# Moving ten steps of each row's relu experts from the second part of a slot to the first part of the next

## The chip, the cores and the metric

The kernel runs on one core of one Trainium2 chip. The metric is the device time of one execution in microseconds (us). TensorE is called PE here, VectorE DVE, ScalarE ACT, GpSimd POOL and SyncE SP, as in the profile. All data are 32 bit floats.

## The reference, cut to what matters

The input is a batch of 4 rows of 512 tokens with 128 channels. Two layers follow each other. Each adds an attention and a mixture of experts to its input, both taken from the same layer norm:

```python
xn = _layernorm(x, axis=-1)
x = x + _L0_attn_ref(xn, ...) + _L0_ffn_ref(xn, ...)
xn = _layernorm(x, axis=-1)
x = x + _L1_attn_ref(xn, ...) + _L1_ffn_ref(xn, ...)
```

The first attention is banded: for 16 heads each token looks back at 64 tokens, through two GELU networks on differences of projections. The first layer's experts are 16 gated ones, of which a token uses 4. The second attention is full, with 16 heads of 8 channels over the row's 512 tokens. The second layer's experts, the "relu experts" of this study, are these:

```python
for e in range(N_EXPERTS):            # 8
    h = jax.nn.relu(xf @ W1[e] + b1[e])   # 128 -> 512
    y = h @ W2[e] + b2[e]                 # 512 -> 128
    out = out + gate[:, e:e + 1] * y
```

All experts are computed for every token, and the gate of those that the router doesn't choose is zero.

## The kernel before, in words

The work is written as Python generators, the tracks. A track issues some instructions and yields; what lies between two yields is a step. `woven` runs several tracks side by side: each comes with a quota, and the track that is least far on in its share of the quota does the next step. A track leaves when it ends or when it has used up its quota, and it can be taken up again later. A scheduler then sets the final order of the instructions on each engine. It starts from the order written, looks at which tiles are free, and can move instructions past each other; matmuls of the scores, of `lbank` (L586) and of the second attention's weighting (L879) have a high priority in it. On the chip each engine works through its own queue in order.

The first layer goes through four slots, one for each row b. A slot has two parts, and each is one `weave`:

- `band_logits(b)` has 66 steps, 64 of which subtract two windows on DVE (L572, the tile `z`), apply GELU on ACT (L574, L578), and multiply on PE with four column tiles side by side (L586, into `lbank`). The last step writes the exponentials `e` (L628, L632) to a table `by_t` in HBM (L633). 30 steps are in the first part (24 for row 0), the others in the second.
- `gated_experts(b)` has 16 experts with two matmuls of 128x512 (L686, L693) and four pairs of 128x128 (L675).
- `band_values(b - 1)`, in the first part, reads `by_t` (L312), transposes (L321), writes to a second table `by_s` (L327), reads that in another shape (L339) and multiplies with the values (L353, L357).
- `prepare(b + 1)`, in the second part, makes the next row's layer norm, projections and routes.
- `relu_experts(b - 1)` starts in the second part of slot b and goes on in the first part of slot b + 1. It needs the whole first layer of row b - 1.

`relu_experts` has 43 steps in the slots. Six make the layer norm, the transpose (L235), the router (four matmuls of `hidden`, L388, and 16 small ones, L418), the routes and `total`. 36 steps belong to nine passes of four: in each of them one `hidden` of expert e (L388 on PE, then a relu on ACT, L396) and one product of expert e - 1 (L454). At the head of a pass come the loads of the two weights and of the route (L440, L442, L444, all issued by SP, into tiles with two buffers each), at its end a product on DVE (L458) and a sum on POOL (L459). The last step adds the sum to the row. In the attention stage a step of `hidden` and one of L454 are apart, so what is left of a row there counts twice.

After the four slots comes the attention stage. `full_attention` works on pairs of score matmuls: in each of its inner steps one pair of heads is multiplied for the maxima (L966, then L983 on DVE) and one pair for the weights (L966, then the exponential L990 on ACT), and in between come the products with the values (L879), transposes (L815) and projections. Its score matmuls are held in a written order, the list `pace`, and the experts' `hidden` is tied to it. Beside it run, in this order, `band_values` of the last row together with the rest of row 2's relu experts, and then all of row 3's.

Of the kernel before, what the change touches and what calls it, by code (L numbers as in the profile page):

```python
# [29 lines left out]
B, T, C = 4, 512, 128  # L30
# [49 lines left out]
def woven(*tracks):  # L80


    live = [[g, n, 0] for g, n in tracks]
    while live:
        t = min(live, key=lambda v: (v[2] + 1) / v[1])
        t[2] += 1
        if next(t[0], "end") == "end" or t[2] == t[1]:
            live.remove(t)
        yield
# [8 lines left out]
def two_layers(ctx: ExitStack, tc: tile.TileContext, w: dict, consts: bass.AP, out: bass.AP):  # L98
# [8 lines left out]
    def bank():  # L107
        return ps_f.tile([P, 512], FP, tag="f", name="bank")
# [16 lines left out]
    def c_(name):  # L125
        return cst[:, offs[name][0]:offs[name][1]]
# [80 lines left out]
    def layernorm(b, dst, pin=False):  # L207

        mv = small.tile([P, TPB, 2], FP, tag="mv", name="mv")
        for i in range(TPB):  # L210
            st = small.tile([P, 6], FP, tag="st", name="st")
            ins = nc.vector.bn_stats(st, x1[:, b * TPB + i, :])
            if pin and not i:
                tc.keep_in_program_order(ins)
            nc.vector.bn_aggr(mv[:, i, :], st)
        rs = inv_sqrt(mv[:, :, 1], 1.0)
        for i in range(TPB):
            nc.vector.tensor_scalar(
                dst[:, i, :], x1[:, b * TPB + i, :], mv[:, i, 0:1], rs[:, i:i + 1],
                ALU.subtract, ALU.mult,  # L220
            )
# [9 lines left out]
    def transposed(src):  # L231

        pt = bank()
        for i in range(TPB):
            nc.tensor.transpose(pt[:, i * P:(i + 1) * P], src[:, i, :], ident)  # L235
        return pt

    def routes(pool, tag, g, n, k, less, dst):


        shape = [P, TPB, n, n]
        both = pool.tile([P, 2, TPB, n * n], FP, tag=tag, name="both")
        gt, eq = both[:, 0], both[:, 1]
        other = g[:, :, None, :].to_broadcast(shape)
        own = g[:, :, :, None].to_broadcast(shape)
        gt4 = gt.rearrange("p t (a b) -> p t a b", a=n)
        eq4 = eq.rearrange("p t (a b) -> p t a b", a=n)
        nc.vector.tensor_tensor(gt4, other, own, ALU.is_gt)
        nc.vector.tensor_tensor(eq4, other, own, ALU.is_equal)
        nc.vector.tensor_tensor(eq, eq, less[:, None, :].to_broadcast([P, TPB, n * n]), ALU.mult)  # L250
        nc.vector.tensor_tensor(gt, gt, eq, ALU.add)
        rank = small.tile([P, TPB, n], FP, tag=f"rank{n}", name="rank")
        nc.vector.tensor_reduce(rank, gt4, AX.X, ALU.add)
        nc.vector.tensor_scalar(rank, rank, float(k), None, ALU.is_lt)
        mx = small.tile([P, TPB], FP, tag="rmx", name="rmx")
        nc.vector.tensor_reduce(mx, g, AX.X, ALU.max)
        nc.vector.tensor_tensor(dst, g, mx[:, :, None].to_broadcast([P, TPB, n]), ALU.subtract)
        nc.scalar.activation(dst, dst, AF.Exp)
        nc.vector.tensor_tensor(dst, dst, rank, ALU.mult)
        nc.vector.tensor_reduce(mx, dst, AX.X, ALU.add)  # L260
        nc.vector.reciprocal(mx, mx)
        nc.vector.tensor_tensor(dst, dst, mx[:, :, None].to_broadcast([P, TPB, n]), ALU.mult)
# [18 lines left out]
    def add_rows(b, py):  # L281
        nc.vector.tensor_tensor(rows_of(b), rows_of(b), py, ALU.add)
# [102 lines left out]
    def hidden(wt, bias, b, c):  # L385

        ph = bank()
        mm = nc.tensor.matmul(ph, wt[:, c * P:(c + 1) * P], xT[:, b * T:(b + 1) * T], start=True, stop=True)  # L388
        if pace:
            tc.add_manual_dep(  # L390
                mm.ins, pace[-1].ins.name,
                mybir.DependencyInfo(mybir.DependencyClass.NoSync, mybir.DependencyReason.DATA),
                reason="experts spread over the steps",
            )
        h = chain.tile([P, T], FP, tag="h", name="h", bufs=5)
        nc.scalar.activation(h, ph, AF.Relu, bias=bias[:, c:c + 1])  # L396
        return h

    def relu_experts(b):


        xn = chain.tile([P, TPB, C], FP, tag="o", name="xn", bufs=1)
        rw1 = chain.tile([C, F1], FP, tag="ew1", name="rw1")
        nc.sync.dma_start(out=rw1, in_=w["L1_ffn_rw1"])
        layernorm(b, xn)
        yield
        pt = transposed(xn)
        nc.scalar.copy(xT[:, b * T:(b + 1) * T], pt)
        yield
        hs = []  # L410
        for c in range(4):
            hs.append(hidden(rw1, cols[:, 32:36], b, c))
            if c % 2:
                yield
        pg = bank()
        for i in range(TPB):
            for c in range(4):
                nc.tensor.matmul(  # L418
                    pg[:, i * E1:(i + 1) * E1], hs[c][:, i * P:(i + 1) * P], rw2[:, c, :],
                    start=(c == 0), stop=(c == 3),  # L420
                )
        scores = small.tile([P, TPB, E1], FP, tag="scores1", name="scores1")
        nc.vector.tensor_tensor(
            scores, pg[:, :TPB * E1].rearrange("p (t e) -> p t e", e=E1),
            rb2[:, None, :].to_broadcast([P, TPB, E1]), ALU.add,
        )
        route = small.tile([P, TPB, E1], FP, tag="route1", name="route1")
        routes(small, "pairs", scores, E1, K1, c_("lt8"), route)
        yield
        rT = route_rows(small, route, E1, route_d[1][b], 1.0)  # L430
        py = bank()
        nc.tensor.matmul(py, b2_1, rT, start=True, stop=True)
        total = chain.tile([C, T], FP, tag="total", name="total", bufs=1)
        nc.scalar.copy(total, py)
        yield
        old = None
        for e in range(E1 + 1):
            if e < E1:
                w1 = chain.tile([C, F1], FP, tag="ew1", name="ew1")
                nc.sync.dma_start(out=w1, in_=w["L1_ffn_W1"][e])  # L440
                w2 = chain.tile([P, 4, C], FP, tag="ew2", name="ew2")
                nc.sync.dma_start(out=w2, in_=w["L1_ffn_W2"][e].rearrange("(c p) d -> p c d", p=P))  # L442
                r = chain.tile([P, T], FP, tag="r", name="r")
                nc.sync.dma_start(out=r, in_=route_d[1][b][e].partition_broadcast(P))  # L444
            new = []
            if old:
                py = bank()
            for c in range(4):
                if e < E1:
                    new.append(hidden(w1, cols[:, e * 4:e * 4 + 4], b, c))  # L450
                if pace:
                    yield
                if old:
                    nc.tensor.matmul(py, old[1][:, c, :], old[0][c], start=(c == 0), stop=(c == 3))  # L454
                yield
            if old:
                part = chain.tile([C, T], FP, tag="part", name="part", bufs=1)
                nc.vector.tensor_tensor(part, py, old[2], ALU.mult)  # L458
                nc.gpsimd.tensor_tensor(total, total, part, ALU.add)  # L459
            old = (new, w2, r)  # L460
        pt = transposed(total.rearrange("p (t c) -> p t c", t=TPB))
        add_rows(b, pt)
        yield

    def after(*parts):
        for p in parts:
            yield from p


    with ExitStack() as l0:  # L470
# [31 lines left out]
        ready = {}  # L502
# [227 lines left out]
        experts = {}  # L730
        for b in range(B):
            logits_b, gated_b = band_logits(b), gated_experts(b)
            if not b:
                weave((logits_b, 6), (preparation, 4))
            first = [(logits_b, 30 if b else 24), (gated_b, 7)]
            second = [(logits_b, 37), (gated_b, 10)]
            if b:
                first.append((band_values(b - 1, ready[b - 1][1]), 23))
                experts[b - 1] = relu_experts(b - 1)
                second.append((experts[b - 1], 22))  # L740
            if b > 1:
                first.append((experts[b - 2], 22))
            if b + 1 < B:
                second.append((prepare(b + 1), 6))
            weave(*first)
            weave(*second)
# [45 lines left out]
    def full_attention():  # L792
# [204 lines left out]
    x_out = out.rearrange("b (t p) c -> p b t c", p=P)  # L997
    weave(
        (full_attention(), 106),
        (after(woven((band_values(B - 1, ready[B - 1][1]), 23), (experts[B - 2], 42)), relu_experts(B - 1)), 22 + 42 + 79 + 4),  # L1000
    )
    nc.sync.dma_start(out=x_out[:, B - 1], in_=x1[:, (B - 1) * TPB:B * TPB, :])

# [33 lines left out]
```

## Time and profile before

| what | value |
|---|---|
| median of 3 runs | 1337.98 us (1337.77 to 1341.17) |
| the profiled execution | 1343.06 us |
| its span, first to last instruction | 1341.3 us |
| PE matmul busy | 1144.2 us, 85% |
| PE weight load busy | 441.0 us, 33% |
| DVE busy | 1008.7 us, 75% |
| ACT busy | 1007.8 us, 75% |
| POOL busy | 94.6 us, 7% |
| mean granted clock of PE | 0.939 |
| DMA | 120.75 MB, mean 90 GB/s |

The profiled execution is one run with the hardware profiler, and all durations and waits come from it. Its time differs from the median of the runs, so a sum of durations is made against its own time. Busy shares are averages over the slots and the attention stage, which have different limits; they have to be read stage by stage. Matmuls are pipelined: the end of one is modelled, and the distance between the starts of two tells more about PE's pace than the duration of one. A 32 bit matmul shows as two records.

### The profile page before, as it was taken

The page shows a single profiled execution, that of the slowest core. Times are in us where ns is not written, and L with a number is a line of the kernel's source. Part 1 is how long each engine was busy: PE and PEld are TensorE (multiplying, and loading weights), DVE is VectorE, ACT ScalarE, POOL GpSimd, SP SyncE. Part 2 cuts the span into 40 slices and gives each one's busy share as a digit, 9 for nine tenths or more (in the row PEclk, how much of TensorE's full clock was granted, in tenths as well). Part 3 has the DMA queues.
Part 4 walks back from the last instruction along what each step waited for, and adds up shares of the span by engine and source line. Part 5 has one row for each costly group of instructions (what it writes and reads, how often), then busy time and mean ns, then how long its engine had stood idle before and what let it go on. Part 6 is the DMA issues. An engine that isn't in the chain of part 4 may idle for free. (4 is left out here: it accounts for less than half of the span.)

```text
span 1341.3 us, 17381 instructions
## 1 busy us (share of the span) xinstructions
PE 1144.2 (85%) x6727; PEld 441.0 (33%) x6727; DVE 1008.7 (75%) x1085; ACT 1007.8 (75%) x1141; POOL 94.6 (7%) x72
## 2 busy tenths in 40 slices
PE   5686876677899969987987899897899989999996
PEld 2122323122444413334432344333333333333332
DVE  4999998999977899998689999864555546445451
ACT  4899997989878899999888999884254535544544
POOL 2000000000000100300010310002300000000000
PEclk9799888878989989999998999899899989999999
DMA  8122211455322445542233564224453130120100
GB/s 276 42 72 59 72 56 54 133 116 124 88 72 63 157 106 125 146 111 64 68 125 104 134 159 121 63 75 135 117 111 101 40 87 9 35 68 32 48 24 9
DMA packets 170348, 120.75 MB, mean 90 GB/s; under 512 B 66909, under 2 KB 149562, under 8 KB 168730
## 3 DMA queue, kind: packets, MB, share of 16 engines
q1 hardware_dynamic: 168794, 112.91, 31.0%
q0 software_dynamic: 1184, 6.29, 1.2%
q8 instruction: 54, 0.88, 0.3%
q10 hardware_dynamic: 288, 0.43, 0.1%
q14 instruction: 28, 0.23, 0.1%
HBM read 90.57 MB, written 29.03 MB: 89 GB/s over the span
## 5 line engine op out<-in xcount | busy, mean ns | idle before, releaser
L572 DVE TENSOR_TENSOR z<-proj 128x2044 f32<-128x2044 f32 (+31 forms) x256 | 554.3, 2188 | 28.4 <-PE lbank L586 18.5
L586 PE MATMUL lbank<-z,place 128*32 128x504 f32 (+18 forms) x2048 | 295.6, 651 | 107.4 <-ACT z L578 63.2
L983 DVE TENSOR_REDUCE nmax<-score 128x2 f32<-128x1024 f32 x128 | 156.3, 1225 | 174.3 <-PE score L966 166.6
L578 ACT ACTIVATE z<-z,posb 128x1024 f32<-128x1024 f32 (+31 forms) x256 | 266.7, 1097 | 9.2 <-DVE z L572 7.4
L574 ACT ACTIVATE z<-z,brep 128x2048 f32<-128x2048 f32 (+31 forms) x128 | 241.5, 1904 | 9.5 <-DVE z L572 8.4
L990 ACT ACTIVATE ex<-score 128x1024 f32<-128x1024 f32 x128 | 130.4, 1023 | 145.3 <-PE score L966 145.2
L459 POOL TENSOR_TENSOR total<-total,part 128x512 f32<-128x512 f32 x32 | 73.3, 2289 | 1022.1 <-DVE part L458 996.2
L388 PE MATMUL bank<-xT,ew 128*128 128x512 f32 x256 | 138.3, 632 | 6.1 <-DVE e L628 5.7
L454 PE MATMUL bank<-h,ew 128*128 128x512 f32 x256 | 134.1, 623 | 2.6 <-ACT h L396 2.6
L396 ACT ACTIVATE h<-bank,cols 128x512 f32<-128x512 f32 x144 | 98.0, 685 | 45.7 <-PE bank L388 45.0
L586 PEld LDWEIGHTS lbank<-z,place 128*32 128x32 f32 x2048 | 44.6, 113 | 264.2 <-ACT z L578 129.2
L966 PE MATMUL score<-kpad,qpad 32*128 32x512 f32 x384 | 109.9, 645 | 4.1 <-DVE nmax L983 3.2
L966 PE MATMUL score<-qa,kpad 32*128 32x512 f32 x384 | 103.6, 648 | 2.2 <-ACT ex L990 2.2
L675 PEld LDWEIGHTS accbank<-wT,lin 128*128 128x128 f32 x512 | 72.0, 206 | 64.7 <-issue 37.3
L675 PE MATMUL accbank<-wT,lin 128*128 128x128 f32 x512 | 83.9, 303 | 8.4 <-DVE lin L673 8.2
L686 PE MATMUL gbank<-tT,wT 128*128 128x512 f32 x128 | 70.6, 633 | 18.9 <-DMA wT<-wT_all 18.2
L879 PE MATMUL accbank<-ex,vaug 128*32 128x512 f32 x512 | 70.3, 615 | 0.2 <-ACT ex L990 0.2
L693 PE MATMUL gbank<-tT,wT 128*128 128x512 f32 x128 | 67.6, 610 | 0.0
L689 ACT ACTIVATE glu<-gbank,gbt 128x512 f32<-128x512 f32 x64 | 43.8, 685 | 28.4 <-PE gbank L686 28.0
L388 PEld LDWEIGHTS bank<-xT,ew 128*128 128x128 f32 x256 | 41.9, 194 | 69.5 <-issue 52.7
L454 PEld LDWEIGHTS bank<-h,ew 128*128 128x128 f32 x256 | 44.1, 195 | 62.6 <-issue 50.6
L671 DVE SCALAR_TENSOR_TENSOR lin<-lin,r 128x512 f32<-128x512 f32 x64 | 45.7, 714 | 13.4 <-ACT lin L695 13.1
(198 smaller groups left out, 1223.5 us busy)
## 6 DMA issues: line engine op xcount, KB each, us to landing
r<-route SPq DMA_DIRECT2D x96, 256.0 KB
ew<-in_L_ffn_W SPq DMA_DIRECT2D x64, 256.0 KB
wb<-by_s SPq DMA_DIRECT2D x32, 512.0 KB
wT<-wT_all SPq DMA_DIRECT2D x48, 192.0 KB
by_t<-e SPq DMA_DIRECT2D x8, 1024.0 KB
f<-by_t SPq DMA_DIRECT2D x128, 64.0 KB
by_s<-g SPq DMA_DIRECT2D x16, 512.0 KB
wb<-by_s SPq DMA_DIRECT2D x24, 256.0 KB
```

Source lines behind the costliest of these rows:

```text
L388: mm = nc.tensor.matmul(ph, wt[:, c * P:(c + 1) * P], xT[:, b * T:(b + 1) * T], start=True, stop=True)
L396: nc.scalar.activation(h, ph, AF.Relu, bias=bias[:, c:c + 1])
L454: nc.tensor.matmul(py, old[1][:, c, :], old[0][c], start=(c == 0), stop=(c == 3))
L459: nc.gpsimd.tensor_tensor(total, total, part, ALU.add)
L572: nc.vector.tensor_tensor(z[:, :, :, 0:n], seen, own, ALU.subtract)
L574: nc.scalar.activation(z[:, :, :, 0:n], z[:, :, :, 0:n], AF.Gelu, bias=b_dmg)
L578: last = nc.scalar.activation(z[:, dq, :, 0:n], z[:, dq, :, 0:n], AF.Gelu, bias=posb[:, j:j + 1])
L586: mm = nc.tensor.matmul(ps[q:q + 32, t0:T], place[:, kind, 3 - dd:35 - dd], z[:, dq, hg, 0:n], start=(dd == 0), stop=(dd == 3),)
L675: nc.tensor.matmul(ya[:, i * P:(i + 1) * P], lin[:, i * P:(i + 1) * P], wT[:, 2, :], start=False, stop=(e == E0 - 1 and i == TPB - 1),)
L966: mm = nc.tensor.matmul(ps[:, h - two, :], own[r, i * P:(i + 1) * P], seen[r, :], start=True, stop=True)
L983: freed.append(nc.vector.tensor_reduce(nmax[n % 2][:, i, two:two + 2, 8:9], ps, AX.X, ALU.max, negate=True))
L990: freed.append(nc.scalar.activation(ex[n, i][:, two:two + 2, :], ps, AF.Exp, scale=inv))
```

## The change

The quotas of `relu_experts` in the `weave` calls are other ones:

```diff
                 experts[b - 1] = relu_experts(b - 1)
-                second.append((experts[b - 1], 22))
+                second.append((experts[b - 1], 12))
             if b > 1:
-                first.append((experts[b - 2], 22))
+                first.append((experts[b - 2], 33))
...
-        (after(woven((band_values(B - 1, ready[B - 1][1]), 23), (experts[B - 2], 42)), relu_experts(B - 1)), 22 + 42 + 79 + 4),
+        (after(woven((band_values(B - 1, ready[B - 1][1]), 23), (experts[B - 2], 62)), relu_experts(B - 1)), 22 + 62 + 79 + 4),
```

Of a row's 43 steps 12 instead of 22 are written into the second part of the slot that follows the row's own. These are the six steps ahead of the experts and one and a half passes, where it was four passes. The other 31 instead of 21 steps are written into the first part of the slot after that, and for row 2, which has no such slot, into the attention stage (62 instead of 42, as steps there count twice). The quota of the attention stage's second track grows by the same 20, so that it still ends with `full_attention`. Row 3's experts stay where they were. No instruction is added or removed.

## The prediction

> **What bounds the kernel now.** I read the page's 40 slices first: VectorE (DVE) and ScalarE (ACT) are full until slice 28 and half empty after it, while TensorE (PE) is full at the end. So I asked for the busy time of each engine in stretches, cut where a slot starts, where its first part ends (its 30th z subtraction, L572) and at the first score (L966, 941.7 us). Two lines for each of slots 0 to 3, first and second part, then the attention stage ("tail"):
>
> ```profile
> core 0: us, PE busy (x) PEld busy (x) DVE busy (x) ACT busy (x) POOL busy (x), PEclk, DMA share, GB/s
> 23.40:111.20 87.80, 63.52 (x354) 21.67 (x354) 84.84 (x70) 80.95 (x92) 0.00 (x0) 0.86 0.26 78
> 111.20:233.50 122.30, 91.55 (x506) 34.99 (x504) 114.10 (x128) 109.40 (x132) 0.11 (x1) 0.89 0.18 56
> 233.50:310.00 76.50, 49.55 (x376) 16.12 (x376) 74.07 (x53) 71.86 (x64) 0.00 (x0) 0.86 0.47 120
> 310.00:461.20 151.20, 136.19 (x771) 61.38 (x772) 127.39 (x165) 129.18 (x155) 7.26 (x4) 0.93 0.34 91
> 461.20:543.20 82.00, 68.25 (x426) 23.28 (x425) 78.78 (x57) 76.50 (x73) 6.45 (x3) 0.90 0.46 127
> 543.20:699.30 156.10, 140.22 (x792) 62.36 (x788) 129.99 (x165) 138.95 (x167) 18.28 (x6) 0.99 0.37 100
> 699.30:781.60 82.30, 66.61 (x422) 23.62 (x422) 77.90 (x56) 75.77 (x71) 14.88 (x2) 0.90 0.44 125
> 781.60:941.70 160.10, 143.89 (x771) 60.94 (x767) 119.42 (x137) 127.49 (x150) 17.58 (x11) 0.96 0.38 112
> 941.70:1341.30 399.60, 374.44 (x2296) 130.79 (x2296) 195.62 (x233) 192.35 (x231) 21.58 (x20) 0.97 0.23 56
> ```
>
> First parts are DVE's (74.07 of 76.50, 78.78 of 82.00, 77.90 of 82.30) and leave PE idle for 14 to 27 us. Second parts are PE's (136.19 of 151.20), with DVE idle for 24 to 41 us. The tail is PE's alone. The change thus takes matmuls from where PE binds to where it does not, three times, and the last time it drops them into the tail. Then I read PE's timeline in both places. In slot 1's second part it is packed; a 128x512 f32 matmul is two records and costs 0.86 us (433.28 to 435.03 below: 0.89, then 0.86):
>
> ```profile
> 433.28 1.05 PE L675 MATMUL accbank<-wT,lin 128*128 128x128 f32 x8
> 434.17 1.02 PE L388 MATMUL bank<-xT,ew 128*128 128x512 f32 x2
> 435.03 1.02 PE L454 MATMUL bank<-h,ew 128*128 128x512 f32 x2
> ```
>
> In the tail it is a row of steps, each with eight score records:
>
> ```profile
> 1166.58 0.70 PE L966 MATMUL score<-kpad,qpad 32*128 32x512 f32 x2
> ...
> 1167.65 1.06 PE L879 MATMUL accbank<-ex,vaug 128*32 128x512 f32 x8
> 1168.64 1.12 PE L388 MATMUL bank<-xT,ew 128*128 128x512 f32 x2
> 1169.70 0.70 PE L966 MATMUL score<-kpad,qpad 32*128 32x512 f32 x2
> ...
> 1170.93 1.02 PE L454 MATMUL bank<-h,ew 128*128 128x512 f32 x2
> 1172.25 0.70 PE L966 MATMUL score<-kpad,qpad 32*128 32x512 f32 x2 [0.29 <-DVE nmax L983]
> ```
>
> The step with L879 and an expert's matmul takes 3.12 us (1166.58 to 1169.70) and is full. The next, with one matmul, takes 2.55 and ends in a wait for DVE. A step with L879 and no expert's matmul takes 2.54 too (1149.65 to 1152.19), one with two 512 wide matmuls and no L879 2.98 (1186.49 to 1189.47). So 2.55 is the floor that scores and maxima set, and room in a step is free.
>
> **What moves.** Nothing is added or removed. Of 43 steps of a row, ten move on: five hidden matmuls (L388) with their relus, about five of L454 for each pair of experts, with one or two L458 products, and the weight loads (L440, L442, L444) of an expert or so. A scheduler sets the final order, so I counted both programs' PE orders between the same z matmuls (L388 plus L454): slot 1 second part 30 to 9; slot 2 first 25 to 38, second 42 to 33; slot 3 first 26 to 35, from there to the first score 52 to 44; tail 97 to 113. Sixteen matmuls more lie in the tail, not the twenty that the step numbers say, because the rows lag behind their steps. All other work stays, but for small shifts.
>
> **Slot 1, second part.** 21 matmuls x 0.90 (0.86 and a little for changing shape) = 18.9 us leave PE, 9 relus x 0.69 = 6 us leave ACT, two products x 0.69 leave DVE. PE falls to 117, DVE to 126, ACT to 123. At the share that DVE reached in slot 0's second part, which has no experts (114.10 of 122.30, 93%), 126 makes 135: a gain of 16. At the present share (84%) it is 150: a gain of 2. I take 12, near the first, since PE is the releaser of 13.5 of DVE's 22 us of idle time from 362 to 475, but the row's start (layernorm, routes) is a chain that stays.
>
> At this place the Trainium skill speaks against the reading. "Perfetto Trace Analysis", section Identifying the Most-Contended Engine, says that busy matmuls are a bad measure for TensorE and that weight-load share is a better one; here that share is 61.38 of 151.20, 41%, which would leave ACT with 129.18 as the most contended. By it only the relus count, this gain would be 6 and the sum below 6 us worse. I hold to the record starts 0.86 apart without a gap, which say that PE's queue is full.
>
> **Slot 2, first part.** 13 more, 11.7 us of PE, which then has 80 of 82 us. The nearest price: slot 1's first part without experts took 76.5, this one with 25 matmuls 82.0, 0.22 each, so 13 cost 2.9. If PE becomes the bound at the 90% that it reaches in second parts (136.19 of 151.20), 80 makes 89, a cost of 7. I take +4. **Second part:** 9 fewer. The price from slot 1's second part to this (12 more matmuls, 4.9 us) is 0.41, a gain of 3.7; at full price 8. I take -4. **Slot 3, first part:** 9 more, 2.0 at 0.22, 6 at PE's 90% or so; PE has 74.7 of 82.3, so +3. **To the first score:** 8 fewer, between 0 and -7.2. The last 15 us before the score are a chain of landings (by_t, then w_qkv) that no matmul shortens: -4. Together these five make -12 + 4 - 4 + 3 - 4 = **-13**.
>
> In the first parts more loads stand in SP's queue, each waiting for PE to free a weight buffer, with band_values' reads (L312, L339) behind them. I cost that at nothing as the reads have several steps of lead; without that cover see the third rival.
>
> **Tail.** I price each step of both orders by the rows above: 2.55, or, where it is more, 1.27 us (1.41 with L879) plus 0.853 for each 512 wide matmul and its share for the rest. The order of before sums to 368 and that of after to 388: **+20**. It is above 16 x 0.86 = 13.8 because six steps, not one, have matmuls between their two pairs of scores; the one before took 6.15 us (1200.81 to 1206.96), where four matmuls behind the scores would make 1.41 + 4 x 0.86 = 4.85. Against it stands this wait:
>
> ```profile
> 1076.77 0.66 PE L353 MATMUL bank<-wb,va 128*32 128x128 f32 x8 [4.51 <-DMA wb<-by_s]
> ```
>
> The write to by_s was issued at 1068.21, 8.6 us earlier, 3.4 steps. After puts three to four steps between the two everywhere; before has two here and five or eight elsewhere. So 4.5 goes, and smaller waits may come at the others: -1. Tail: **+19**, from +5 (16 x 0.57 = 9.1 for filling free room, less 4.5) to +24 (16 x 1.06, what the chain of waits shows for one such matmul between scores, plus five splits x 1.3).
>
> **Sum.** -13 + 19 = +6 on the profiled execution's 1343.06 (span 1341.3 and 1.8 around it) makes 1349.1. That run lies 5.1 above the median of 1337.98, so the forecast for the median is **1344**. Within 0.3% means within 4 us, about what a measurement of this kernel can tell from no change.
>
> **Rivals.**
> - *The slots give more than the tail takes: 1329.* Slot 1's second part falls to DVE's bound (-16), the others give +3, -6, +2, -6, together -23, and the tail takes 14 (16 x 0.86, as the wait at L353 pays for the splits). For it: PE's packed timeline and DVE's 24 to 41 us idle. Against it: the low price of 0.41 between slots 1 and 2. It decides once the slots give more than the tail takes by 4. Chance 0.30.
> - *They cancel: 1337.* The slots give 18, the tail takes 17. Chance 0.25. Here belongs also that the change does little of what it says, the rows lagging behind their steps.
> - *First parts stall: 1354.* A weight load that waits for PE holds L339 back in SP's queue, PE waits at L353 in front of the z matmuls, and DVE runs out of buffers. With the 4.5 us of the wait above once in each of two first parts, +9 or 10 on the forecast. The DMA share of 0.46 and DVE's 4% of idle time speak against it. Chance 0.07.
> - *The forecast, 1344.* Chance 0.38; its own range is 1342 to 1352.
>
> Faster 0.30, same 0.25, slower 0.38 + 0.07 = 0.45. The ends of all terms together reach from -23 to +33 but will not meet; 1327 to 1355 leaves out about two in ten.
>
> **What would show it.** The first score should come near 929 us, from 941.7; slot 1's second part near 139 us long, slot 2's first near 86; the tail near 419, from 399.6, with the gap at L353 under 2 us. A first score before 922 would speak for the first rival. A tail less than 14 us longer would show the price of the steps wrong, an unchanged second part of slot 1 that PE was not its bound.

## The result and the profile after

| | before | after |
|---|---|---|
| median of 22 runs each | 1338.58 us (1334.05 to 1343.51) | 1344.80 us (1335.65 to 1349.38) |
| ratio | | 1.0043 [1.0031, 1.0055] |
| the profiled execution | 1343.06 us | 1342.70 us |
| its span | 1341.3 us | 1340.2 us |
| first score (L966) | 941.7 us | 924.8 us |
| PE matmul busy | 1144.2 us | 1148.5 us |

The change costs 6.2 us, by the interval 4.1 to 7.4. The two profiled executions hide this: that of before was 4.5 above its median, that of after 2.1 below. So the medians carry the result, and the profiles tell only where time moved. These are the nine stretches of the kernel after, cut at the same places as those of before (columns: the stretch and its length, busy time of PE, PE's weight loads, DVE, ACT and POOL with the number of instructions, the granted clock of PE, the DMA share, GB/s):

```profile
21.40:109.00 87.60, 62.80 (x354) 21.33 (x354) 84.90 (x71) 81.05 (x92) 0.00 (x0) 0.86 0.29 83
109.00:231.00 122.00, 91.21 (x506) 34.90 (x504) 113.95 (x128) 109.15 (x132) 0.11 (x1) 0.89 0.18 56
231.00:307.40 76.40, 49.34 (x376) 16.07 (x376) 73.83 (x52) 71.92 (x64) 0.00 (x0) 0.86 0.46 120
307.40:444.00 136.60, 116.22 (x723) 52.28 (x724) 123.19 (x161) 120.04 (x141) 1.38 (x2) 0.93 0.32 86
444.00:526.70 82.70, 72.87 (x436) 24.43 (x434) 79.18 (x56) 79.92 (x80) 6.12 (x3) 0.94 0.50 140
526.70:684.80 158.10, 143.36 (x796) 64.25 (x792) 132.24 (x170) 136.46 (x164) 12.32 (x5) 0.94 0.34 94
684.80:765.40 80.60, 70.01 (x427) 23.73 (x428) 77.67 (x56) 76.91 (x74) 12.91 (x3) 0.92 0.51 140
765.40:924.80 159.40, 138.68 (x767) 59.62 (x765) 123.59 (x137) 127.33 (x149) 26.04 (x14) 0.96 0.38 111
924.80:1340.20 415.40, 394.26 (x2328) 138.70 (x2328) 196.55 (x235) 198.17 (x239) 19.80 (x18) 0.98 0.22 56
```

Three rows hold the story. In slot 1's second part (307.40) PE lost 20 us of work and the part 14.6 us. In slot 2's second part (526.70) PE has fewer expert matmuls, nine by the prediction's way of counting, and yet is busy for 143.36, where before it was 140.22; the part is 2.0 longer. The row itself tells why the nine bring no relief: it holds 796 records of PE, and that of before 792. In this stretch PE's trace has 72 expert records (two to a matmul) instead of 86, but eight more of L675, eight more of L586 and two more of L693, which came in across the stretch's ends. And PE was at half clock for 20.5 us of it, before for 3.4. The tail (last row) is 15.8 longer, and PE's busy time there grew by 19.8. The wait of 4.51 us before L353 is gone: the view of this line lists what PE waited for ahead of it from 268 us to 1107 us, and the transfer to `wb` ended 0.8 us of idle time in all:

```profile
L353 PE MATMUL bank<-wb,va x512: 269/273/421, 268.4 to 1107.5; 128*32 128x128 f32 x171
...
  DMA wb<-by_s: 0.8, 2
```

A single profile varies by several us, so I also compare every execution that has the same PE order in a stage, but for the unread matmuls that some have; the experiments gave many. "Before's order" and "after's order" below mean those. Lengths in us:

| stage | before's order | after's order | difference | forecast |
|---|---|---|---|---|
| slot 1, second part | 151.2 to 152.1 (5 executions) | 136.4 to 136.9 (8) | -15.3 | -12 |
| slot 2, first part | 78.2 to 78.7 (4), and 81.8 in the profile of before | 82.7 to 82.8 (8) | +4.3 to the four | +4 |
| slot 2, second part | 158.1 to 158.2 (3), and 156.1 to 156.3 | 158.1 to 159.7 (3) | +1.0 to the three | -4 |
| slot 3, first part | 81.0 to 81.2 (3), and 82.3 | 80.5 to 81.4 (7) | -0.4 to the three | +3 |
| to the first score | 160.1 in the profile, 160.3 and 163.3 | 159.4 in the profile, 156.0 and 156.3 | -0.7 in the profiles, -2.9 with all three of after's order to the profile of before | -4 |
| tail | 397.1 to 401.7 (7) | 415.4, 416.6, and twice 413.4 | +16.2 with the first two, +14.9 with all | +19 |

With the first value in each of the last two rows the differences (of the means) sum to +5.1, within the interval of the medians; with the second they sum to +1.6. The two executions that make this difference belong to kernels of the experiments and lay 5.6 and 2.8 us below the medians of these kernels. So the stages add up to the total only within some 3 us, and the medians alone carry it. The 81.8 in slot 2's first part goes with the clock: PE was at half clock for 17.1 us of it, in the four others for 3.4 to 6.8.

### The profile page after: what moved, and what is told of

Same layout as the page of the kernel before. It is cut to its first block, busy times and chain, and to the rows that moved or that the text cites. A ratio compares the mean times of both kernels' runs of the same rounds, so it can differ in the third digit from the quotient of the medians.

```text
span 1340.2 us, 17386 instructions
## 1 busy us (share of the span) xinstructions
PE 1148.5 (86%) x6727; PEld 441.0 (33%) x6727; DVE 1011.7 (75%) x1085; ACT 1006.3 (75%) x1141; POOL 87.2 (7%) x72
## 4 chain that ended last, share of the span: by engine, by line
PE 61%; ACT 19%; DVE 11%; issue 5%; DMA 3%; POOL 0%; SPq 0%; POOLq 0%; DVEq 0%
PE lbank L586 11%; PE score L966 11%; PE bank L388 9%; PE bank L454 7%; ACT z L578 7%; DVE z L572 5%; ACT z L574 4%; PE accbank L879 4%; PE gbank L686 3%; PE accbank L675 3%; PE gbank L693 2%; DVE nmax L983 2%; DMA wT<-wT_all 1%; PE abank L815 1%; ACT lin L695 1%
## 5 line engine op out<-in xcount | busy, mean ns | idle before, releaser
L586 PE MATMUL lbank<-z,place 128*32 128x504 f32 (+18 forms) x2048 | 295.4, 651 | 100.2 <-ACT z L578 56.0
L983 DVE TENSOR_REDUCE nmax<-score 128x2 f32<-128x1024 f32 x128 | 156.3, 1225 | 186.6 <-PE score L966 186.4
L388 PE MATMUL bank<-xT,ew 128*128 128x512 f32 x256 | 137.4, 622 | 6.4 <-DVE e L628 3.4
L586 PEld LDWEIGHTS lbank<-z,place 128*32 128x32 f32 x2048 | 43.9, 114 | 263.0 <-ACT z L578 118.9
L459 POOL TENSOR_TENSOR total<-total,part 128x512 f32<-128x512 f32 x32 | 65.7, 2054 | 811.3 <-DVE part L458 767.0
L966 PE MATMUL score<-kpad,qpad 32*128 32x512 f32 x384 | 110.7, 648 | 3.5 <-ACT ex L990 1.3
L966 PE MATMUL score<-qa,kpad 32*128 32x512 f32 x384 | 104.1, 651 | 2.2 <-ACT ex L990 2.2
L675 PE MATMUL accbank<-wT,lin 128*128 128x128 f32 x512 | 86.1, 304 | 19.7 <-DVE lin L673 19.7
L675 PEld LDWEIGHTS accbank<-wT,lin 128*128 128x128 f32 x512 | 72.7, 207 | 78.8 <-issue 36.2
L686 PE MATMUL gbank<-tT,wT 128*128 128x512 f32 x128 | 72.8, 651 | 17.1 <-DMA wT<-wT_all 16.5
L693 PE MATMUL gbank<-tT,wT 128*128 128x512 f32 x128 | 69.1, 622 | 0.0
L388 PEld LDWEIGHTS bank<-xT,ew 128*128 128x128 f32 x256 | 40.4, 190 | 66.7 <-issue 47.9
L689 ACT ACTIVATE glu<-gbank,gbt 128x512 f32<-128x512 f32 x64 | 43.7, 683 | 20.7 <-PE gbank L686 20.3
```

Of the source, the lines that this page charges most:

```text
L586: mm = nc.tensor.matmul(ps[q:q + 32, t0:T], place[:, kind, 3 - dd:35 - dd], z[:, dq, hg, 0:n], start=(dd == 0), stop=(dd == 3),)
L675: nc.tensor.matmul(ya[:, i * P:(i + 1) * P], lin[:, i * P:(i + 1) * P], wT[:, 2, :], start=False, stop=(e == E0 - 1 and i == TPB - 1),)
L686: nc.tensor.matmul(pg, wT[:, 0, :], tT, start=True, stop=True)
L966: mm = nc.tensor.matmul(ps[:, h - two, :], own[r, i * P:(i + 1) * P], seen[r, :], start=True, stop=True)
L983: freed.append(nc.vector.tensor_reduce(nmax[n % 2][:, i, two:two + 2, 8:9], ps, AX.X, ALU.max, negate=True))
```

## The experiments

The theory at the start was the prediction's: PE gains where it binds, first parts take matmuls cheaply, and the tail takes back more than the slots gave. So without the tail's share the change should be faster. The rival: a row's work that is put off is paid for wherever it comes back, and the slots together give little. The rows' quotas are tried first, then the waits ahead of the attention stage and in it, then the clock. "Row r" is `relu_experts(r)`; it starts in the second part of slot r + 1. Ratios are to the kernel before, run beside it.

**The rows alone.** The first kernel shortens rows 0 and 1 and leaves row 2, whose steps would fall into the tail, as before:

```diff
-                second.append((experts[b - 1], 22))
+                second.append((experts[b - 1], 12 if b < 3 else 22))
-                first.append((experts[b - 2], 22))
+                first.append((experts[b - 2], 33))
```

> Rows 0 and 1 moved as in the change, row 2 as before (22 steps in slot 3, 42 in the attention stage). TensorE's order then has the 97 expert matmuls of before in the attention stage and 60 instead of 52 between slot 3's first part and the first score. My theory (the slots give, the attention stage takes): slot 1's second part about 14 us shorter, slots 2 and 3 together 3 to 6 us longer, the attention stage unchanged: 8 to 11 us below before, near 1329. Rival (the first parts of slots 2 and 3 stall behind weight loads, and this makes the loss): as much as the change or more above before, 1344 or later.

Measured: 1337.61 us against 1337.17, ratio 1.0013 [0.9999, 1.0028]. The tail is 397.1, so row 2 is the tail's price, but neither the gain expected nor the rival's loss came: the 15 us of slot 1 are given back before the first score (935.5).

The next three move one row each. Row 2 alone (`22 if b < 3 else 12` in the second part, 62 instead of 42 in the attention stage):

> Only row 2 moved: 36 instead of 52 expert matmuls between slot 3's first part and the first score, 113 instead of 97 in the attention stage, with the order of the attention stage as in the change. My theory: the stretch before the first score 7 to 10 us shorter (16 x 0.5 to 0.6), the attention stage 16 to 19 longer: 7 to 11 above before, near 1347. Rival (first parts stall): no first part is touched, so within 3 us of before or faster.

Measured: 1349.09, ratio 1.0085 [1.0064, 1.0105], as expected: 7 gained before the first score (153.2), 17 lost in the tail (416.6).

Row 0 alone (`12 if b == 1 else 22`, and `33 if b == 2 else 22` in the first part):

> Only row 0 moved: slot 1's second part has 9 expert matmuls instead of 30, slot 2's first part 38 instead of 25, its second part 50 instead of 42, slot 3's first 31 instead of 26, the rest to the first score 47 instead of 52; the attention stage is that of before. My theory: slot 1's second part 14 us shorter, slot 2's first part +1 to +4, its second +3 to +4, the rest about 0: 7 to 11 us below before, near 1329. Rival (first parts stall): slot 2's first part takes back 10 us or more, no gain.

Measured: 1345.92, ratio 1.0064 [1.0045, 1.0083]. The expectation fell. Slot 1's second part gave its 15, slot 2's first part took its 4, and slot 2's second part took 12, where 3 to 4 were expected.

Row 1 alone (`12 if b == 2 else 22`, `33 if b == 3 else 22`):

> Only row 1 moved: slot 2's second part has 22 instead of 42 expert matmuls, slot 3's first part 38 instead of 26, the rest to the first score 60 instead of 52; slot 1 and the attention stage are those of before. My theory, by the prices of the prediction (0.4, 0.2 and 0.5 us each): -8 + 3 + 4, about 1 us below before, 1334 to 1341. If slot 2's second part is bound by TensorE as slot 1's is (0.7 us for each of its matmuls): -14 + 3 + 4 = -7, near 1331. Rival (first parts stall): above before by 3 us or more.

Measured: 1348.29, ratio 1.0077 [1.0052, 1.0102]. It fell in the same way: slot 2's second part gave 7, slot 3's first took 2, the stage to the first score took 14, where 4 were expected.

These are slot 2's second part with row 0 late, then with row 1 short, in the views by stage of the two kernels:

```profile
526.10:696.30 170.20, 154.82 (x830) 67.78 (x826) 133.51 (x171) 141.21 (x171) 16.34 (x7) 0.96 0.34 96
```

```profile
538.40:689.20 150.80, 131.71 (x754) 58.59 (x751) 128.06 (x163) 129.46 (x152) 8.89 (x4) 0.92 0.33 91
```

And the stage to the first score with row 1 late, then with row 2 short:

```profile
772.30:946.60 174.30, 156.15 (x800) 64.44 (x796) 123.17 (x139) 134.44 (x157) 21.15 (x12) 0.93 0.36 105
```

```profile
777.00:930.20 153.20, 131.79 (x738) 55.78 (x734) 118.70 (x135) 121.68 (x142) 19.34 (x13) 0.93 0.38 111
```

Put into a two by two table, they give the mechanism:

| | slot 2, second part | to the first score |
|---|---|---|
| as before | 158 | 160 |
| earlier row late only | 170.2 | 174.3; 168.0 and 173.3 (rows 0 and 1 moved, the second with unread matmuls in slot 2) |
| own row short only | 150.8 | 153.2 |
| both, as in the change | 158.1 to 159.7 | 156.0 to 159.4 |

A row that is cut short gives 7 in its second part. The same row is late by then: it runs past the first part where it should have ended, and the next second part pays 8 to 14 for its rest. In the change each of those parts has a late row and a short one, and they cancel. Only the first part of the chain (slot 1, -15) and its end (tail, +16) stay. PE's busy time moves with the lengths in these rows (131.71, 154.82, 156.15, 131.79), and its idle time stays near 15 to 21 us, which points to PE's work. A step that moves takes its relu on ACT along, and ACT's busy time moves too (from 129.46 to 141.21 in the first two), so this is not a test of PE alone. The one kernel that adds work of PE alone in a packed place is the control further below: there 5.1 us of it made the part 1.4 to 3.0 us longer.

**Half of the shift.** If only the amount was wrong, a smaller step might keep the gain. Row 0 alone, moved by five steps (`17 if b == 1 else 22`, `27 if b == 2 else 22`); counted as in the prediction, between the same z matmuls, PE's order has the same 42 expert matmuls in slot 2's second part as before:

> Row 0 alone, moved by five steps instead of ten. Slot 1's second part then has 19 expert matmuls instead of 30, slot 2's first part 35 instead of 25, and slot 2's second part 42, as before (with ten steps it had 50 and took 170 us instead of 156 to 158). Theory: what row 0's move lost was the overflow into slot 2's second part, so here slot 1's second part is 7 to 9 us shorter, slot 2's first part 3 to 4 longer, the rest that of before: 3 to 6 us below before, 1331 to 1335. Rival (rows that are written later delay whatever stands behind them, overflow or not): at or above before, 1337 or later.

Measured: 1351.00, ratio 1.0099 [1.0084, 1.0113], the worst of all. Slot 1's second part gave 8.6, but slot 2's second part is 165.6:

```profile
534.40:700.00 165.60, 150.25 (x814) 67.25 (x813) 133.53 (x169) 139.72 (x168) 9.81 (x6) 0.95 0.34 97
```

PE is 10 us busier there than in the profile of before. So the count that the prediction relied on doesn't tell the load, and the trace shows what it leaves out: in this stretch, from one z subtraction to another, there are 93 expert records instead of 86 and again eight more of L675, eight of L586 and two of L693. At 0.86 for a matmul of two records and 0.9 for a group of eight I estimate 5.7 us for them. PE was at half clock for 17.1 us, before for 3.4, which is enough for the rest. The stage to the first score is 165.8, 6 longer at the same count too; why, no run shows.

**The tail's wait without the tail's work.** Before with the last band_values and row 2's rest interleaved as in the change (`(experts[B - 2], 62)` in the inner call only):

> The kernel before with the quota 62 instead of 42 for row 2 beside the last row's band_values in the attention stage, and nothing else: the same 97 expert matmuls there (96 by order), but band_values' steps lie further apart, as in the change. By order its L353 products come at least four steps behind the transposes, and three steps instead of one are split; the price by steps is 371 instead of 368. Theory: the wait of 4.5 us before L353 goes, the splits cost 3: 1 to 2 us below before, 1335 to 1337. Rival (the change's attention stage was spared by something else, and the wait only moves): the wait stays above 3 us somewhere, 1340 or later.

Measured: 1349.72, ratio 1.0087 [1.0065, 1.0110]. The expectation fell: the wait stayed, as this line of PE's timeline shows, and the tail is 407.6.

```profile
1071.40 0.66 PE L353 MATMUL bank<-wb,va 128*32 128x128 f32 x8 [4.31 <-DMA wb<-by_s]
```

So this kernel doesn't tell what the wait is worth. In its profile an order of the same work alone moved the tail by 8 us, where the priced steps sum to 371 against 368.

**The pause before the first score.** In the change the time from PE's last `hidden` (L388) before the attention stage to the first score grew from 10.45 us (931.25 to 941.70) to 14.83. PE's timeline of before, then of after:

```profile
931.25 1.13 PE L388 MATMUL bank<-xT,ew 128*128 128x512 f32 x2
932.22 1.88 PE L454 MATMUL bank<-h,ew 128*128 128x512 f32 x4
936.84 1.32 PE L850 MATMUL abank<-xT,wqk 128*128 128x512 f32 x2 [2.75 <-DVE wqk L767]
938.84 2.08 PE L859 MATMUL abank<-xT,wqk 128*128 128x512 f32 x2 [0.68 <-ACT q L854]
```

```profile
909.95 1.12 PE L388 MATMUL bank<-xT,ew 128*128 128x512 f32 x2
910.92 1.88 PE L454 MATMUL bank<-h,ew 128*128 128x512 f32 x4
919.18 2.08 PE L850 MATMUL abank<-xT,wqk 128*128 128x512 f32 x2 [6.39 <-DMA f<-by_t]
921.93 2.07 PE L859 MATMUL abank<-xT,wqk 128*128 128x512 f32 x2 [0.68 <-ACT q L854]
924.78 2.09 PE L966 MATMUL score<-k,q 32*128 32x512 f32 x8 [0.78 <-ACT k L863]
```

The bracket holds the idle time and its releaser: 6.39 us instead of 2.75, and L850 takes 2.08 instead of 1.32, which is the half clock. (The landing of `f` that it names fell together with the end of DVE's copies L767, at 919.2; L850's weight load waited 7.2 us for these.) To test the clock I put unread 128x512 matmuls behind the last expert matmul there, seven in the change, three in before (there `3 if (b, e, c) == (2, 4, 2)`); they go to a bank that nothing reads:

```diff
+        for idle in [bank()] * n if n else []: tc.add_manual_dep(nc.tensor.matmul(idle, ident, xT[:, 0:T], start=True, stop=True).ins, mm.ins.name, dep, reason="fill")
...
-                yield
+                yield fill(mm, 7 if (b, e, c) == (2, 2, 2) else 0)
```

> The change, with seven more matmuls of 128x512 that nobody reads, put behind the last expert matmul before the attention stage, where TensorE waits 6.4 us for landings and then runs its first products at half the granted clock. Work is added, none left out. Theory (the pause lowers the clock): the first products at full clock, the time from the write to by_t to the first scores and the first steps after it 2 to 4 us shorter, 1341 to 1343 if the change is 1344.8. Rival (the landings alone set it, or the added 6 us of TensorE count): same as the change within 1 us, or 3 to 6 above it.

> The kernel before, with three such matmuls at the same place; there the pause is 2.75 us, and the first products and scores run at half the granted clock for 13.7 us. Theory (the pause lowers the clock): the first scores' steps take 2.6 to 3 us each instead of 5.2 and 5.0 (with their parts of 1 us at 0.5 each), 3 to 5 us below before, 1333 to 1335. Rival: same as before within 1 us, or 2 above.

Measured: the change so filled takes 1337.37, ratio to before 0.9993 [0.9981, 1.0006], against 1.0043 [1.0031, 1.0055] without: about 7 us less with 6 us more work on PE. Before so filled takes 1339.69, 1.0013 [1.0002, 1.0023]: no gain. In the filled change L850 starts 6.3 us after the last L388, not 9.2, and the records are at full clock:

```profile
914.63 1.12 PE L388 MATMUL bank<-xT,ew 128*128 128x512 f32 x2
915.59 1.02 PE L454 MATMUL bank<-h,ew 128*128 128x512 f32 x2
916.53 4.56 PE L400 MATMUL bank<-xT,cst 128*128 128x512 f32 x10
920.93 1.02 PE L850 MATMUL abank<-xT,wqk 128*128 128x512 f32 x2
```

The clock is not all of it. L850 waits for two copies on DVE (L767) and these waited for POOL. DVE's timeline of before, of after, and of the filled change:

```profile
935.96 0.89 DVE L767 COPY wqk<-w_qkv 128x128 f32<-128x128 f32 x2 [1.08 <-DMA w_out<-in_L_attn_w_out]
```

```profile
916.51 2.68 DVE L767 COPY wqk<-w_qkv 128x128 f32<-128x128 f32 x2 [2.93 <-DMA w_out<-in_L_attn_w_out]
```

```profile
917.08 0.54 DVE L767 COPY wqk<-w_qkv 128x128 f32<-128x128 f32 x2 [11.23 <-DMA w_qkv<-in_L_attn_w_qkv]
```

The same two copies take 0.89, 2.68 and 0.54. In after they begin at 916.51 in the middle of a POOL copy and end at 919.19, just after a POOL memset:

```profile
915.41 1.89 POOL L777 COPY kpad<-cst 128x2048 f32<-128x2048 f32 x1
917.24 1.81 POOL L776 MEMSET qpad<- 128x2048 f32 x1
918.99 1.95 POOL L777 COPY kpad<-cst 128x2048 f32<-128x2048 f32 x1
```

In the filled change they begin at 917.08, late in a memset that ends at 917.47, and are done at 917.62. So where these copies fall among POOL's work is worth 2.1 us here. No run moved POOL's memsets alone, so this share is read from the times and not tested.

The whole chain can be read in more executions, from the last issue of the write to `by_t` (L633) to the second step of scores. It takes 23.6 to 24.3 us in the four kernels that have row 2 short and not the seven matmuls, and 20.4 and 19.9 in the two that have both (the second kernel stands below). In before it takes 20.9 and in before so filled 20.7. So the seven take 3 to 4 us off this chain, and where the rest of the 7 lies is not known. DVE's first maxima of the scores tell why before had nothing to gain. These are they in before, in before so filled, and in the change:

```profile
944.41 2.36 DVE L983 TENSOR_REDUCE nmax<-score 128x2 f32<-128x1024 f32 x2 [7.55 <-POOL nmax L787]
```

```profile
941.05 2.36 DVE L983 TENSOR_REDUCE nmax<-score 128x2 f32<-128x1024 f32 x2 [6.61 <-POOL nmax L787]
```

```profile
927.04 2.36 DVE L983 TENSOR_REDUCE nmax<-score 128x2 f32<-128x1024 f32 x2 [7.84 <-PE score L966]
```

In before the maxima wait for POOL's memset of `nmax` (L787) and not for PE. The filling brings the first score forward there, from 15.7 us after the write to 14.5, and the maxima still wait for POOL. In the change they wait for PE's scores, so an earlier score counts.

The tail of the filled change is 3.1 shorter (412.3) than in the profile of the change. 1.1 of it is in the first step, as its records are at full clock (the eight of L966: 1.14 instead of 2.09). The rest is no more than the tails of this order differ among each other (413.4 to 416.6).

**The clock in slot 2's second part.** The clock column stood out there: 0.94 after, 0.99 before. By the clock records PE was at half clock for 20.5 us there (3.4 at 600.6, 6.8 at 624.5, 10.2 at 655.2), before for 3.4. This is PE's timeline of after around the last stretch:

```profile
652.10 1.02 PE L388 MATMUL bank<-xT,ew 128*128 128x512 f32 x2
655.51 2.08 PE L675 MATMUL accbank<-wT,lin 128*128 128x128 f32 x8 [2.40 <-DVE lin L673]
660.05 2.04 PE L686 MATMUL gbank<-tT,wT 128*128 128x512 f32 x2 [2.46 <-DMA wT<-wT_all]
661.89 1.91 PE L693 MATMUL gbank<-tT,wT 128*128 128x512 f32 x2
```

Two pauses of 2.4 us, and the records from 655.51 to 665 take about twice their time (L693 1.91, elsewhere 1.02). The stretch at 624.5 has no pause ahead of it. PE is busy there without a gap, mostly with the router's narrow matmuls (L418, 8 columns):

```profile
620.60 2.07 PE L418 MATMUL bank<-rw,h 128*128 128x8 f32 x18
622.60 0.98 PE L586 MATMUL lbank<-z,place 128*32 128x462 f32 x8
623.51 2.33 PE L418 MATMUL bank<-rw,h 128*128 128x8 f32 x14
```

Six unread matmuls were put into the change, two ahead of L686 of expert 8 and four ahead of that of expert 15; the control has all six at expert 11, where no pause lay:

```diff
-                pg = ps_g.tile([P, T], FP, tag="g", name="gbank")
+                pg = ps_g.tile([P, T], FP, tag="g", name="gbank"); [nc.tensor.matmul(pg, ident, tT, start=True, stop=True) for _ in range({8: 2, 15: 4}.get(e, 0) if b == 2 else 0)]
```

> The change with six 128x512 matmuls more, whose result nobody reads (each is overwritten by the gated matmul L686 that follows it in the same bank). They stand in the order where PE paused in slot 2's second part in the changed kernel's profile: two ahead of L686 of expert 8 (pause of 1.49 us) and four about the last pauses (2.40 us before L675 and 2.46 before L686 of expert 15). The rest of PE's order is the changed kernel's. Theory: half clock after half-empty windows took back what the experts' matmuls gave up here. Then the 20.5 us of half clock in this part fall to 10 or less, the part is 3 to 6 us shorter than 158.1, and the kernel comes to 1338 to 1341, 3 to 6 below the change. Rival: the clock only follows the waits and costs nothing, PE's added 5 us lie in the pauses or lengthen them: 158 to 162 long, 1344 to 1348.

> The control to the six unread matmuls: the same six, all ahead of L686 of expert 11 of slot 2, where PE's order was packed and no pause lay. Theory (what counts is where the pauses are): the pauses ahead of experts 8 and 15 stay, the half clock stays near 20 us, the part is 2 to 5 us longer than 158.1, the kernel 1346 to 1350. Rival (any more work on PE in this part lifts the clock, or it does not matter): as with the pauses filled, within 2 us of that kernel.

Measured: 1342.12, ratio 1.0029 [1.0013, 1.0045], and for the control 1341.54, 1.0030 [1.0014, 1.0047]. Slot 2's second part in the two:

```profile
527.00:683.70 156.70, 141.66 (x808) 61.68 (x804) 132.11 (x170) 136.61 (x164) 12.31 (x5) 0.99 0.33 95
```

```profile
526.00:687.10 161.10, 147.91 (x808) 64.80 (x804) 132.89 (x170) 136.39 (x164) 12.33 (x5) 0.95 0.33 92
```

In these two profiles the clock did as expected: 0.99, 3.4 us at half clock against 17.1 in the control, and PE is 6.3 us less busy at the same work. But the next two kernels hold the same six matmuls and don't repeat it: there this part was at half clock for 17.1 us and 161.5 long, like the control, and for 10.2 us and 158.1 long. So that the pauses set the clock here is not shown. In the first profile the part is only 1.4 shorter than in the change, less than the 3 to 6 expected; six unread matmuls cost 5.1 us themselves (x 0.86), and the pauses moved, as here in PE's timeline of the filled kernel:

```profile
656.99 1.12 PE L686 MATMUL gbank<-tT,wT 128*128 128x512 f32 x2 [1.50 <-DMA wT<-wT_all]
657.95 1.02 PE L693 MATMUL gbank<-tT,wT 128*128 128x512 f32 x2
661.81 1.43 PE L586 MATMUL lbank<-z,place 128*32 128x456 f32 x8 [2.84 <-ACT z L578]
```

The whole kernel is no different from the control. So the theory that the half clock of this part explains the loss doesn't hold for the total: the part differs by 4.4 us between these two profiles, and the totals by nothing that shows. Both medians are some 3 us below the change's, with intervals that overlap its 1.0031 to 1.0055.

Both fillings together, and the pauses filled in the kernel with only rows 0 and 1 moved:

> The change with both fillings: six unread matmuls in the pauses of slot 2's second part and the seven ahead of the first score. If the pauses are separate causes, the gains add: 7.4 below the change from the seven, and 3 to 6 more from the six, so 1331 to 1335, below the kernel before by 0.2 to 0.5%. If the six do nothing, 1337 as with the seven alone. If both act through the same thing (the clock's windows shifted), less than the seven alone.

> Rows 0 and 1 moved and row 2 left as before (which gave 1337.6 against 1337.2), with the six unread matmuls in the pauses of slot 2's second part, where PE's order is the changed kernel's. Theory: 3 to 6 us from the clock there, so 1332 to 1335, and the second part 154 to 157 long where it was 159.6. Rival: no gain, 1337 to 1340, as what the part saves is waited for later (slot 3's second part, 168 long, has the rows' work that was pushed back).

Measured: 1339.27, ratio 1.0013 [0.9998, 1.0028], and 1341.78, 1.0028 [1.0013, 1.0043]. Neither gains: the first is no better than the seven alone (beside the kernel with the six alone the seven take off 2.9 us, with intervals that overlap), the second, if anything, worse than without the filling (1.0013). No version here beats the kernel before.

## Why the prediction was right, point by point

The sign and the size came out: 1344.0 forecast, 1344.8 measured. The steps behind it were right at both ends and wrong in between.

- *Slot 1's second part, -12.* It is -15.3, near the bound of 16. PE's busy time fell by 20.0 and its idle time rose by 5.4 (15.0 to 20.4 us); DVE reached 123.19 of 136.60, 90%, where 93% was the bound. The chain at the row's start that was to hold it back costs little. The Trainium skill's rule on the most contended engine ("Perfetto Trace Analysis", section Identifying the Most-Contended Engine), which the prediction set aside, read by its weight-load share alone, would have given a gain of 6 here. The profiles show that the part became 14.6 shorter, while ACT's busy time fell by 9.1, DVE's by 4.2 and PE's by 20.0. The record starts 0.86 us apart were the better guide.
- *Slot 2's first part, +4.* Measured +4.3 against the four executions; the two profiles alone show 0.7 (82.00 to 82.70), as before took longer there in its profile than in the four. So the price of 0.22 for a matmul was read off an execution that had 17.1 us of half clock in this part, and the +4 came out in part by luck.
- *Slot 2's second part, -4.* This step failed: +1.0. It counted 42 matmuls against 33 and priced the difference. Row 1, cut short, does give 7 (150.8 alone), but row 0's late rest takes back 7 to 9. PE is 3.1 us busier than before in this part; in the kernel with the pauses filled, nearly free of half clock, its busy time less the unread 5.1 is 136.5, 3.7 below before. So the steps that came in across the stretch's ends (the groups of L675, L586 and L693 above) and the half clock ate the 7.7 that nine matmuls were to give.
- *Slot 3's first part, +3.* Failed by 3.4: -0.4. The upper bound of 6 doesn't follow from the prediction's own 90%: 74.7 us of PE at 90% make 83.0, which is 0.7 more than 82.3. PE had room for nine matmuls there at no cost; the 0.33 for each that the term stands for was too much.
- *To the first score, -4.* Short by 3 in the profiles and by 1 with the two later executions. PE is 5.2 us less busy in the profile, but the part is 0.7 shorter. The chain of landings, which the prediction took as fixed, grew: from the last issue of the write to `by_t` to the first score it took 15.7 us in before and 18.8 to 19.5 in the four kernels with row 2 short and not the seven. The copies L767 fell among POOL's memsets there, and L850 came late at half clock.
- *Tail, +19.* Measured +16.2. The priced steps gave +20, and PE's busy time in the tail did grow by 19.8. The wait at L353 went nearly wholly (4.5, with 0.8 left) where the prediction allowed 1 net, which fits the smaller loss; no run took the wait away alone. The test for the price of the steps, a tail more than 14 longer, is met in the profile (15.8) and just missed in the two later executions (13.6 above the mean of before's order), so the first rival's 14 is not far off.
- *The sum.* -13 for the slots was -11.1 (-15.3 + 4.3 + 1.0 - 0.4 - 0.7), +19 was +16.2, and so +6 was +5.1 by the table's first values and +6.2 in the medians. Three terms came out about 3 us better than forecast and two 3 and 5 worse; they canceled. That the tail takes back what the slots give was foreseen; that the total came within 1 us is luck.

The first score was forecast near 929 and came at 924.8. Of these 4 us 2.6 lie ahead of slot 1's second part, which began at 307.40 instead of 310.00 and which the change doesn't touch. A score before 922, which would have spoken for the first rival, did not come. *First parts stall* has nothing for it either: they took 82.7 and 80.6, with DVE busy for 79.18 and 77.67.

## What to carry to other kernels

Here moving a row's work out of a full stage made that row late, and the next stage paid for the rest of it; price every stage that the row still crosses, with the lag, and not the one that it leaves. Move one row at a time to see it: here the three cuts alone cost 0.6 to 0.9% each and together 0.4%, so neither signs nor sizes of such edits add up. Where a fraction of a per cent is at stake, compare several executions of each order stage by stage, since single profiles here lay up to 5.6 us from the median of their kernel (1336.47 against 1342.12), and 3.6 apart in one stage of the same order (81.8 against 78.2).

## What the runs showed of the hardware

- The half clock comes in stretches that are multiples of 3.4 us. In executions of the same order they mostly fall at the same places: 600.6 for 3.4, 624.5 for 6.8, 655.2 for 10.2 in the change, 601.1, 625.0 and 659.1 with the same lengths where rows 0 and 1 alone are moved. Not always: in slot 2's first part the order of before had 17.1 us of it in one execution and 3.4 to 6.8 in four. The Trainium skill ("TensorE: Matmul & The Clock Gate", section HAM oscillation — how this bites in real kernels) asks for no idle gaps above some 3.4 us. The trace agrees with the unit but not with the limit: the stretch of 10.2 us at 655.2 began at the end of a gap of 2.40 and holds one of 2.46, and in before one of 6.8 us began at 483.7 within a gap of 2.21, with none above 1.2 in the 7 us ahead of that gap.
- Half clock also followed stretches in which PE was busy without idling. In the fourteen profiles 44 stretches of half clock, from slot 1's second part on, began after 3.4 us in which the records of PE cover 90% or more. In each of them 17 to 31 records of the router's 128x8 matmuls (L418) lie in these 3.4 us. The reverse doesn't hold: the same matmuls in the profile with the pauses filled (from 621.77) were followed by none.
- Filling a pause with work that nobody reads kept the clock up before the first score of the change, and the chain there became 3 to 4 us shorter (24.0 to 20.4) and the kernel about 7. In the same place of before the clock rose too (L850 1.06 instead of 1.32) and nothing was gained, as the maxima there wait for POOL. In slot 2 (six matmuls, 5.1 us) the half clock of the part was 3.4, 10.2 and 17.1 us in three kernels with the same six.
- Two DVE copies of 128x128 from one on-chip tile to another took 0.54 us or 2.68, by where they fell among POOL's memsets and copies of 1.8 to 1.9 us. In all fourteen profiles both copies end 0.08 to 0.15 us after the end of a memset of POOL, and the two together take 0.54 to 3.24 us. The Trainium skill ("SBUF — State Buffer", section Who interferes with whom) says that a DVE copy in a two-port mode and POOL exclude each other for a whole instruction. The times here agree with it, though no trace shows the mode of these copies. A pair that began during a POOL copy (916.51 in the change) also waited for the memset behind it.
